# Graph layer with a residual and a layer norm: VectorE instead of ScalarE copies products of picked rows, placing ahead of the network layer, 64 picked columns per engine and pair of runs

## The chip, the cores and the metric

The kernel runs on one core of one Trainium2 chip. The metric is the device time of one execution in microseconds; a lower one is better. The engines are TensorE (PE, with its weight loads as PEld), VectorE (DVE), ScalarE (ACT), GpSimd (POOL) and SyncE (SP).

## The reference

There are N = 12,500 nodes with 128 features and E = 412,500 directed edges, sorted by their destination. Each edge has four attributes (edge_attr) and eight radial values (edge_scalar_attr).

```
f0 = x0 @ W1_0e / sqrt(32);  f1 = einsum(x1, W1_1o) / sqrt(32)       # per node: 32 scalars, 32 vectors
feat, self = halves of f0 and f1
e0, e1 = feat0[edge_src], feat1[edge_src]                            # rows picked per edge
h = gelu(gelu(radial @ W_mlp1 / sqrt(8)) @ W_mlp2 / sqrt(64))        # per edge: 8 -> 64 -> 64
w00, w01, w10, w11 = h @ Wp_..                                       # 4 x 32 weights per edge
mid = products of w.., e0, e1 and the edge's attributes
n = segment_sum(mid, edge_dst) / sqrt(32)
y = cos * self + sin * (n @ W2 / sqrt(64))
out = layernorm(x + y)                                               # fp32 throughout
```

## The kernel before, in words

The edges are cut into 806 runs of 512 edges (four columns q of 128). Two runs are a *pair* (403 of them, index p), two pairs a *chunk* (202, index c); k = 0 or 1 is the pair's place in its chunk. After a preparation (features of all nodes go to a table in HBM, and x stays transposed in SBUF as xT), one loop over the pairs does everything. The order of PE, ACT, DVE and SP instructions is written out by hand, in the order of the Python code (a manual schedule); the engines run their own lists in order and wait for each other by semaphores. Steps of different pairs are interleaved: while VectorE forms the products of pair p, the networks run for chunk c + 2 and the sums of chunk c - 1 are placed.

In the loop, for pair p:

- `gather` (L223, POOL): for the pair nine ahead, each of the eight columns of 128 rows of the table comes by one indirect DMA into a tile G. There are ten such tiles, so a gather waits for the products of pair p - 1. Some columns come in other ways: `aid` (SP, L208) fetches a column of every 14th run row by row, and *picked* columns are made on the chip.
- *Picked rows.* `copy_columns` copies single columns of xT, at addresses that were read into registers, into a 128x128 tile gt: on VectorE (L188) and on ScalarE (L192), each with its own tile. When a tile is full, `picked_rows` multiplies it by the weights wf (L197, PE, into a PSUM tile of the name h), and ScalarE copies the product into column q of G for the run two pairs ahead (L198). `SLOTS` says how many columns an engine copies at which place of the pair: VectorE has three places, ScalarE four, in pairs with k = 0 and k = 1. Which run gets a product is worked out from the running sums of SLOTS. The function `picks` does one place.
- `segments(p - 1)` (L670, PE) sums the products of the pair before over windows of destinations; `segments_kept` (L676, ACT) copies them out of PSUM as sg.
- `weights(p + 1)` (L597, PE): the per-edge weights of the next pair.
- `mlp1` in pairs with k = 0 and `mlp2` with k = 1 (L554, L570, PE; eight matmuls in the program, two passes each in the profile), with their GELUs on ScalarE (L559, L576), two a layer; `show` (L632, ACT) puts edge attributes into the PSUM bank m between the two GELUs of the first layer.
- `place(c - 1)` for k = 0 (L693 and L697, PE): adds the sums of a chunk's four windows into the same bank m; `add` (L710, DVE) adds that to the node sums acc. `move_sums` (L428, ACT) shifts these sums when a group of 512 nodes is done.
- `messages` (DVE): the products M of a pair in three instructions, part 0 (L650) and parts 1 and 2 (both L654), with picks between them. `select` (L639, DVE, for k = 1) makes the windows S from the shown attributes.
- Groups of nodes that are done go through `moments`, `statistics` and `normalise`.

PSUM tiles of the name h have two buffers, shared by the networks, the products of picked rows, transposes and moments; a matmul into one waits until the tile two before it was read.

Of the kernel before, what the change touches and what calls it, by code (L numbers as in the profile page):

```python
# [8 lines left out]
F32 = mybir.dt.float32  # L9
# [3 lines left out]
AF = mybir.ActivationFunctionType  # L13
OP = mybir.AluOpType
PE = mybir.EngineType.PE
ACT = mybir.EngineType.Activation
DVE = mybir.EngineType.DVE
# [4 lines left out]
P = 128  # L22
# [8 lines left out]
PR = 2  # L31
# [14 lines left out]
AID_FROM = 36  # L46
AID_LEAD = 16
STEPS = 12
SLOTS = {DVE: ((24, 20, 20), (24, 16, 28)), ACT: ((12, 16, 16, 12), (12, 16, 16, 12))}
FROM = {DVE: 6, ACT: 6}  # L50
COL_Q = {DVE: Q - 2, ACT: Q - 3}
A_OF = (1, 2, 3, 0)
# [5 lines left out]
def gnn_kernel(ctx: ExitStack, tc: tile.TileContext, x, src, dst, ea4, ea8, w1_0, w1_1, wm1, wm2,  # L58
# [8 lines left out]
    nc = tc.nc  # L67
# [111 lines left out]
    def copy_columns(e, columns):  # L179

        for at, r in columns:
# [9 lines left out]
            else:  # L191
                nc.scalar.activation(to, col, AF.Copy)  # L192

    def picked_rows(e, i):

        pt = ps.tile([P, P], F32, name="h")
        nc.tensor.matmul(pt, GT.pop((e, i)), wf, start=True, stop=True)  # L197
        nc.scalar.activation(G[picked[e][i]][:, COL_Q[e], :], pt, AF.Copy)  # L198

    def aid(s, t):  # L200

# [387 lines left out]
    def weights(p):  # L589

        c, k = divmod(p, CH // PR)
        runs = [i for i in range(PR) if p * PR + i < NS]
        WP[p] = ps.tile([P, PR, Q, P], F32, name="w")
        for q in range(Q):
            for i in runs:
                rows = slice(i * HID, (i + 1) * HID)
                nc.tensor.matmul(WP[p][:, i, q, :], H2[c][q % 2][rows, k, q // 2, :], wpb[rows, :],  # L597
                                 start=True, stop=True)
# [87 lines left out]
    def place(c):  # L686
        ns = min(CH, NS - c * CH)
        b, r = divmod(c, P)
        _, at = nc.values_load_multi_w_load_instructions(
            run_first[b][r:r + 1, :], engines=[PE], min_val=0, max_val=4 * (SPAN - W),  # L690
            skip_runtime_bounds_check_because="bounded above")
        ST[c] = pt = bank[:, :4 * SPAN].rearrange("p (a n) -> p a n", a=4)
        nc.tensor.matmul(pt.rearrange("p a n -> p (a n)"), none[:, :P], none, start=True, stop=False)  # L693
        to = pt.bitcast(U8)
        for k in range(ns):
            k_at = at[k].with_bounds(guaranteed_mod_val=0, out_of_modulus=4)
            nc.tensor.matmul(to[:, :, bass.ds(k_at, 4 * W)].bitcast(F32), SG[c][:, k, :],  # L697
                             PL[c][:, k, :].rearrange("p (a n) -> p a n", a=4), start=False, stop=k == ns - 1)
# [243 lines left out]
    with tc.manual_schedule(engines={PE, ACT, DVE, SP}):  # L942
# [57 lines left out]
        def picks(e, p, i, op=None):  # L1000
            if p < FROM[e]:
                if op:
                    op()
                return
            n = SLOTS[e][p % (CH // PR)][i]
            if not op:
                copy_columns(e, fetch(e, n))
                return
            first = fetch(e, n // 8 * 4)
            op()  # L1010
            copy_columns(e, first + fetch(e, n - n // 8 * 4))

        for p in range(NP):
            c, k = divmod(p, CH // PR)
            mine = [s for s in range(p * PR, (p + 1) * PR) if s < NS]
            if p:
                for s in mine:
                    if s + LEAD - PR < NS:
                        gather(s + LEAD - PR)
            if k == 1 and c + EDGES_AHEAD < NCH:  # L1020
                load_edges(c + EDGES_AHEAD)
            for s in mine:
                if s % P == P // 2 - 16 and (s // P + 1) * P < NS:
                    load_raws(s // P + 1)
                if s % P == P // 2 and (s // P + 1) * P < NS:
                    load_indices(s // P + 1)
                if s % ET == 8 and s - 8 + ET < NS:
                    load_attributes(s // ET + 1)
                for t in range(P // ROWS):
                    a = s + AID_LEAD - t * STEPS // (P // ROWS)  # L1030
                    if a in aided:
                        aid(a, t)
            nets = c + 2 < NCH
            if k == 0:
                placing(c)
                if c + 1 < NCH:
                    hot_rows(c + 1)
            if p:
                segments(p - 1)
                picks(ACT, p, 0, lambda: segments_kept(p - 1))  # L1040
            for e in picked:
                for s in mine:
                    if (e, s + 2 * PR) in pick_of:
                        picked_rows(e, pick_of[e, s + 2 * PR])
            if k == 1 and c + 3 < NCH:
                radial(c + 3)
            cleared = bool(late)
            rest = list(kept)
            norm_kept()
            picks(ACT, p, 1)  # L1050
            if p + 1 < NP:
                weights(p + 1)
            if nets:
                (mlp1, mlp2)[k](c + 2)
                picks(ACT, p, 2, lambda: (gelu1, gelu2)[k](c + 2, 0))
            else:
                picks(ACT, p, 2)
            if k == 0 and c + 1 < NCH:
                show(c + 1)
            for s in mine:  # L1060
                if s % ET == 20 and s - 20 + ET < NS:
                    turn_attributes(s // ET + 1)
            if nets:
                picks(ACT, p, 3, lambda: (gelu1, gelu2)[k](c + 2, 1))
            else:
                picks(ACT, p, 3)
            if k == 0 and c > 0:
                place(c - 1)
                placed = c
            raws_next = [s + PR for s in mine if s + PR < raw_runs]  # L1070
            for s in raws_next:
                turn_rows(s)
            messages(p, 0)
            if k == 0:
                picks(DVE, p, 0)
            messages(p, 1)
            picks(DVE, p, 1 - k)
            for s in raws_next:
                features(s)
            if rest:  # L1080
                norm_rest()
            if cleared:
                new_sums()
                clearing += list(range(4))
            elif clearing:
                clear_sums(clearing.pop(0))
            if k == 1 and c + 1 < NCH:
                select(c + 1)
            if k == 1:
                picks(DVE, p, 1)  # L1090
            messages(p, 2)
            if k == 1 and placed > added:
                add(added)
                added += 1
            picks(DVE, p, 2)
            if k == 0 and 0 < added == c - 1:
                norm(due.get(added - 1, []))
            if p == 0:
                addresses()
                find_first()  # L1100
                new_sums()
                clearing = list(range(4))
            if p == NP - 4:
                count_odd()
# [52 lines left out]
```

## Time and profile before

| | |
|---|---|
| time of three runs, median (lowest to highest) | 5999.37 us (5995.97 to 6003.86) |
| the profiled execution | 5962.68 us, span 5960.8 us |
| granted TensorE clock, mean | 0.65 |
| matmuls (passes) / column copies on VectorE / on ScalarE | 30,231 / 25,984 / 21,888 |
| gathers / products of picked rows (passes) | 2,722 + 72 / 748 |

The profile is of one execution. The page gives the busy time of each engine as a share of the span; "idle before" of a group of instructions is the time in which their engine did nothing just before them, and the name behind the arrow is what ended it. "issue" means that the profile shows nothing that the engine waited for.

### The profile page before, as it was taken

The page shows a single profiled execution, that of the slowest core. Times are in us where ns is not written, and L with a number is a line of the kernel's source. Part 1 is how long each engine was busy: PE and PEld are TensorE (multiplying, and loading weights), DVE is VectorE, ACT ScalarE, POOL GpSimd, SP SyncE. Part 2 cuts the span into 40 slices and gives each one's busy share as a digit, 9 for nine tenths or more (in the row PEclk, how much of TensorE's full clock was granted, in tenths as well). Part 3 has the DMA queues.
Part 4 walks back from the last instruction along what each step waited for, and adds up shares of the span by engine and source line. Part 5 has one row for each costly group of instructions (what it writes and reads, how often), then busy time and mean ns, then how long its engine had stood idle before and what let it go on. Part 6 is the DMA issues. An engine that isn't in the chain of part 4 may idle for free. (4 is left out here: it accounts for less than half of the span.)

```text
span 5960.8 us, 141936 instructions
## 1 busy us (share of the span) xinstructions
PE 3407.7 (57%) x30231; PEld 2603.1 (44%) x30231; DVE 3366.2 (56%) x28706; ACT 3093.4 (52%) x24111; POOL 2636.3 (44%) x2801
## 2 busy tenths in 40 slices
PE   3665655556555555555556555556655555655556
PEld 2544444444444444444444444444434444443444
DVE  1265656555655555656555665566565555665556
ACT  0254555555555555555555555555554555555554
POOL 4344444444444444444444444444444444444441
PEclk5766666666666666666666666666666666666666
DMA  4211111111111111111111111111111111111111
GB/s 100 59 36 40 39 35 38 41 35 43 42 35 39 39 37 43 40 35 36 36 41 37 40 43 38 37 40 40 41 40 35 35 38 38 40 40 34 40 33 23
DMA packets 576979, 239.04 MB, mean 40 GB/s; under 512 B 481402, under 2 KB 526570, under 8 KB 576106
## 3 DMA queue, kind: packets, MB, share of 16 engines
q0 software_dynamic: 89408, 183.29, 10.8%
q1 hardware_dynamic: 465928, 40.14, 5.4%
q10 hardware_dynamic: 20770, 6.47, 0.5%
q14 instruction: 629, 5.15, 0.3%
q8 instruction: 244, 4.00, 0.3%
HBM read 216.86 MB, written 12.99 MB: 39 GB/s over the span
## 5 line engine op out<-in xcount | busy, mean ns | idle before, releaser
L223 POOL DMA_INDIRECT G<-table,idx x2722 | 2567.2, 943 | 3208.9 <-issue 1313.3
L192 ACT ACTIVATE gt<-xT 128x1 f32 x21888 | 2329.1, 189 | 924.5 <-issue 889.3
L188 DVE COPY gt<-xT 128x1 f32 x25984 | 1891.8, 145 | 1565.0 <-issue 1520.5
L670 PE MATMUL seg<-M,S 128*32 128x128 f32 x12896 | 845.7, 371 | 444.2 <-issue 426.8
L597 PE MATMUL w<-wpb,h 64*128 64x128 f32 x6448 | 855.1, 388 | 383.7 <-issue 383.1
L597 PEld LDWEIGHTS w<-wpb,h 64*128 64x128 f32 x6448 | 699.0, 277 | 554.6 <-issue 544.1
L670 PEld LDWEIGHTS seg<-M,S 128*32 128x32 f32 x12896 | 544.3, 148 | 692.1 <-issue 643.3
L654 DVE TENSOR_TENSOR M<-w,G 128x768 f32<-128x768 f32 x806 | 761.1, 945 | 2.7 <-issue 2.7
L676 ACT ACTIVATE sg<-seg 128x256 f32<-128x256 f32 x403 | 151.1, 375 | 1112.3 <-remote 777.6
L697 PEld LDWEIGHTS m<-pl,sg 128*128 128x128 f32 x1612 | 348.6, 312 | 797.7 <-issue 797.7
L693 PE MATMUL m<-none 128*128 128x384 bf16 x202 | 90.8, 450 | 786.1 <-ACT m L632 412.6
L554 PE MATMUL h<-eT,w1b 64*128 64x128 f32 x3232 | 439.3, 403 | 125.8 <-ACT G L198 95.9
L576 ACT ACTIVATE h<-h 128x512 f32<-128x512 f32 x404 | 237.1, 589 | 491.9 <-remote 377.0
L554 PEld LDWEIGHTS h<-eT,w1b 64*128 64x128 f32 x3232 | 394.3, 303 | 159.5 <-ACT G L198 120.5
L570 PE MATMUL h<-h,w2b 64*64 64x256 f32 x3232 | 393.5, 556 | 105.7 <-ACT G L198 68.7
L197 PE MATMUL h<-wf,gt 128*128 128x128 f32 x748 | 244.0, 411 | 268.2 <-issue 154.2
L650 DVE TENSOR_TENSOR M<-w,G 128x512 f32<-128x512 f32 x403 | 275.5, 684 | 204.1 <-remote 73.9
L697 PE MATMUL m<-pl,sg 128*128 128x128 f32 x1612 | 367.5, 404 | 0.0
L197 PEld LDWEIGHTS h<-wf,gt 128*128 128x128 f32 x748 | 162.8, 263 | 403.6 <-issue 246.9
L639 DVE TENSOR_TENSOR S<-oh,m 128x512 f32<-128x512 f32 x202 | 137.2, 679 | 356.7 <-PE m L697 251.4
L559 ACT ACTIVATE h<-h 128x512 f32<-128x512 f32 x404 | 234.6, 581 | 91.0 <-remote 37.9
L570 PEld LDWEIGHTS h<-h,w2b 64*64 64x64 f32 x3232 | 187.5, 186 | 214.9 <-ACT G L198 87.3
(123 smaller groups left out, 1592.5 us busy)
## 6 DMA issues: line engine op xcount, KB each, us to landing
G<-table SPq DMA_DIRECT2D x7040, 0.5 KB
G<-table,idx POOLq DMA_INDIRECT x2722
e<-in_edge_attr SPq DMA_DIRECT2D x201, 64.0 KB
xt<-in_x SPq DMA_DIRECT2D x24, 256.0 KB
table<-ft ACTq DMA_DIRECT2D x24, 256.0 KB
xt<-in_edge_attr SPq DMA_DIRECT2D x24, 256.0 KB
out<-y SPq DMA_DIRECT2D x24, 256.0 KB
xt<-in_dst SPq DMA_DIRECT2D x5, 256.0 KB
```

Of the source, the lines that this page charges most:

```text
L188: nc.vector.tensor_copy(to, col)
L192: nc.scalar.activation(to, col, AF.Copy)
L197: nc.tensor.matmul(pt, GT.pop((e, i)), wf, start=True, stop=True)
L223: nc.gpsimd.indirect_dma_start(out=G[s][:, q, :], out_offset=None, in_=x if s < raw_runs else table, in_offset=bass.IndirectOffsetOnAxis(a ...
L554: nc.tensor.matmul(p1[h][:, j // 2, j % 2, :], w1b[rows, j, :], eT[c][rows, :], start=True, stop=True)
L570: nc.tensor.matmul(p2[r][k * HID:(k + 1) * HID, h * n:(h + 1) * n], w2b[rows, :], H1[c][h][rows, k * n:(k + 1) * n], start=True, stop=True)
L576: nc.scalar.activation(H2[c][r].rearrange("p k j e -> p (k j e)"), P2[c][r], AF.Gelu_apprx_tanh, scale=1.0 / math.sqrt(HID))
L597: nc.tensor.matmul(WP[p][:, i, q, :], H2[c][q % 2][rows, k, q // 2, :], wpb[rows, :], start=True, stop=True)
L650: nc.vector.tensor_tensor(m[:, :, :, :MUL], w[:, :, :2 * MUL].rearrange("p q (a u) -> p q a u", a=2), g[:, :, None, :MUL].to_broadcast([P, ...
L654: nc.vector.tensor_tensor(m[:, :, j, MUL:].rearrange("p q (i u) -> p q i u", i=3), w[:, :, None, (2 + j) * MUL:(3 + j) * MUL].to_broadcast ...
L670: nc.tensor.matmul(SEG[c][q * W:(q + 1) * W, r + i, :], own[:, (r + i) * Q + q, h * W:(h + 1) * W], M[p][:, i, q, h, :], start=h == 0, sto ...
L697: nc.tensor.matmul(to[:, :, bass.ds(k_at, 4 * W)].bitcast(F32), SG[c][:, k, :], PL[c][:, k, :].rearrange("p (a n) -> p a n", a=4), start=F ...
```

## The change

Three things are changed. VectorE instead of ScalarE copies the products of picked rows out of PSUM, and does so behind part 0 of the pair's messages (with k = 1 behind part 1), while the matmuls stay where they were. `place(c - 1)` stands ahead of `mlp1` in the list of TensorE, no longer behind it and behind `show`. And SLOTS gives both engines 64 columns in each pair: VectorE has 64 and 64 (before 64 and 68), ScalarE 64 and 64 (before 56 and 56). With that each engine fills one tile of 128 in each chunk.

```diff
-SLOTS = {DVE: ((24, 20, 20), (24, 16, 28)), ACT: ((12, 16, 16, 12), (12, 16, 16, 12))}
+SLOTS = {DVE: ((24, 20, 20), (24, 16, 24)), ACT: ((16, 16, 16, 16), (16, 16, 16, 16))}
...
+    PT = {}
+
     def picked_rows(e, i):
 
-        pt = ps.tile([P, P], F32, name="h")
+        PT[e, i] = pt = ps.tile([P, P], F32, name="h")
         nc.tensor.matmul(pt, GT.pop((e, i)), wf, start=True, stop=True)
-        nc.scalar.activation(G[picked[e][i]][:, COL_Q[e], :], pt, AF.Copy)
+
+    def rows_kept(e, i):
+
+        nc.vector.tensor_copy(G[picked[e][i]][:, COL_Q[e], :], PT.pop((e, i)))
...
                 picks(ACT, p, 0, lambda: segments_kept(p - 1))
-            for e in picked:
-                for s in mine:
-                    if (e, s + 2 * PR) in pick_of:
-                        picked_rows(e, pick_of[e, s + 2 * PR])
+            products = [(e, pick_of[e, s + 2 * PR]) for e in picked for s in mine if (e, s + 2 * PR) in pick_of]
+            for e, i in products:
+                picked_rows(e, i)
...
             if p + 1 < NP:
                 weights(p + 1)
+            if k == 0 and c > 0:
+                place(c - 1)
+                placed = c
             if nets:
                 (mlp1, mlp2)[k](c + 2)
                 picks(ACT, p, 2, lambda: (gelu1, gelu2)[k](c + 2, 0))
...
                 picks(ACT, p, 3)
-            if k == 0 and c > 0:
-                place(c - 1)
-                placed = c
...
             messages(p, 0)
+            if k == 1:
+                messages(p, 1)
+            for e, i in products:
+                rows_kept(e, i)
+            picks(DVE, p, 0)
             if k == 0:
-                picks(DVE, p, 0)
-            messages(p, 1)
-            picks(DVE, p, 1 - k)
+                messages(p, 1)
+                picks(DVE, p, 1)
```

Lines of the changed kernel: the products' matmul is L199, VectorE's copy of them L203, the placing L698 and L702, messages L655 and L659, S L644, segments L675, sg L681, gathers L228.

## The prediction

> **What bounds the kernel now.** I read the page first, then the groups by line, the waits, and one stretch of the timeline with all engines beside each other.
>
> ```profile
> span 5960.8 us, 141936 instructions
> PE 3407.7 (57%) x30231; PEld 2603.1 (44%) x30231; DVE 3366.2 (56%) x28706; ACT 3093.4 (52%) x24111; POOL 2636.3 (44%) x2801
> ...
> L223 POOL DMA_INDIRECT G<-table,idx x2722 | 2567.2, 943 | 3208.9 <-issue 1313.3
> L192 ACT ACTIVATE gt<-xT 128x1 f32 x21888 | 2329.1, 189 | 924.5 <-issue 889.3
> L188 DVE COPY gt<-xT 128x1 f32 x25984 | 1891.8, 145 | 1565.0 <-issue 1520.5
> ```
>
> No engine is busy more than 57% of the span. The two groups of column copies (gt) are the largest of ScalarE and VectorE, and both have long idle time whose releaser is "issue": the engine waited for nothing that is shown. The timeline says when that is. Its columns: start, length, engine, line, operation, tiles, count, and in brackets the idle time before.
>
> ```profile
> 2996.15 0.94 DVE L654 TENSOR_TENSOR M<-w,G 128x768 f32<-128x768 f32 x1
> ...
> 3008.28 0.38 ACT L676 ACTIVATE sg<-seg 128x256 f32<-128x256 f32 x1 [0.20 <-remote]
> ...
> 3009.41 1.30 DVE L188 COPY gt<-xT 128x1 f32 x20
> ...
> 3010.63 0.95 DVE L654 TENSOR_TENSOR M<-w,G 128x768 f32<-128x768 f32 x1
> ...
> 3012.34 0.94 POOL L223 DMA_INDIRECT G<-table,idx  x1 [6.04 <-issue]
> ...
> 3012.81 0.57 ACT L559 ACTIVATE h<-h 128x512 f32<-128x512 f32 x1
> ...
> 3013.58 0.94 POOL L223 DMA_INDIRECT G<-table,idx  x1 [0.30 <-issue]
> ...
> 3016.64 0.21 DVE L188 COPY gt<-xT 128x1 f32 x2 [0.55 <-issue]
> 3016.70 0.48 PE L693 MATMUL m<-none 128*128 128x384 bf16 x1 [4.13 <-ACT h L559]
> 3016.97 1.91 PE L697 MATMUL m<-pl,sg 128*128 128x128 f32 x8
> 3018.06 0.21 DVE L188 COPY gt<-xT 128x1 f32 x2 [1.21 <-issue]
> 3018.81 1.94 PE L670 MATMUL seg<-M,S 128*32 128x128 f32 x32
> 3019.48 0.22 DVE L188 COPY gt<-xT 128x1 f32 x2 [1.20 <-PE m L697]
> 3019.83 0.94 POOL L223 DMA_INDIRECT G<-table,idx  x1 [0.30 <-issue]
> ...
> 3022.34 0.69 DVE L639 TENSOR_TENSOR S<-oh,m 128x512 f32<-128x512 f32 x1 [0.55 <-issue]
> ...
> 3023.92 0.94 DVE L654 TENSOR_TENSOR M<-w,G 128x768 f32<-128x768 f32 x1
> ```
>
> GpSimd issues the gathers of a pair in a burst, one every 0.94 + 0.30 = 1.24 us (3012.34 to 3019.83, seven). The burst starts 0.8 us after VectorE's last product M of a pair (3011.58), which frees the buffer. Some 3 to 4 us into it VectorE falls to two copies in 1.4 us (3016.64, 3018.06, 3019.48), where it made 20 in 1.30 us before; this ends some 2 us behind the burst. I call it the slow stretch, and there are two in a chunk of two pairs. Outside it VectorE runs nearly without a gap: from 3009.41 to 3011.58 copies and M touch. So VectorE sets the pace, and a chunk here takes 3024.86 - 2997.09 = 27.8 us (ends of the two L654 that close a chunk).
>
> One row in the slow stretch matters for what follows: TensorE made 32 matmuls in 1.94 us at 3018.81, at full rate, after it had stood 4.13 us at L693. An engine that has waited finds its next instructions at hand, so a wait inside the slow stretch costs less than its length.
>
> **The waits the change touches.**
>
> ```profile
> PE m L693 <- ACT m L632: 412.6, 114, 10.9
> ...
> DVE S L639 <- PE m L697: 251.4, 69, 9.3
> ...
> DVE acc L710 <- ACT acc L428: 169.6, 15, 18.2
> ...
> DVE S L639 <- remote: 67.4, 14, 7.1
> ```
>
> TensorE stands at the placing (L693) until ScalarE has written the shown attributes (L632); the segments of the next pair queue behind it; VectorE's S (L639) waits for the placing.
>
> **Part 1, fewer gathers.** Each engine now picks 64 columns in either pair of a chunk, which fill exactly one tile of 128. The changed program has 393 products instead of 374, and 2775 gathers instead of 2794. 19 gathers at 1.24 us are 24 us of bursts; in them the engines made some progress, so between 0 and -24; I take -20.
>
> **Part 2, VectorE's work.** 25,984 columns become 25,216: 768 fewer, at 1.30/20 = 0.065 us, -50 us. It gains 393 copies of 128x128 out of PSUM. The nearest row is its own copy of that shape from the same kind of tile, 279 ns; ScalarE's copy that goes took 257 ns.
>
> ```profile
> L198 ACT ACTIVATE G<-h 128x128 f32<-128x128 f32 x374 | 87.6, 257 | 4.3 <-PE h L197 4.0 <-remote 0.3
> ...
> L479 DVE COPY colv<-h 128x128 f32<-128x128 f32 (+1 forms) x7 | 1.9, 279 | 5.9 <-PE h L478 3.7 <-issue 2.2
> ```
>
> 393 x 0.279 = +110 us, so the part is +60 us where VectorE runs free; nothing (0) if all of it falls into slow stretches, where the supply of instructions is the limit. I take +60.
>
> **Part 3, placing ahead of the network layer.** L693 no longer stands behind ScalarE's L632, so the waits of S, 251.4 + 67.4 = 319 us, can go, and the segments of the second pair can come 4.1 us sooner (the wait at 3016.70). What is late next for S is L632 itself. -319 is one end, 0 the other; S stands at the end of a slow stretch (3022.34), where a wait costs less than its length, and I take a third, -110 us. The 169.6 us at L710 hang on a move of sums on ScalarE that is not moved; 0. The price of the order: the first network layer (16 matmuls) now stands behind the placing, 3018.81 - 3016.70 = 2.1 us, so its GELU on ScalarE (L559, at 3012.81) comes later by about that.
>
> **Part 4, ScalarE's work.** 21,888 columns become 25,088, 16 more in a chunk. A batch of 16 took 1.59 us (row below): +1.6 us a chunk. Two copies of 0.257 go: -0.5 us. ScalarE is off the path as long as nobody waits for its end; it sat idle 777.6 us at L676 alone, and that covers it:
>
> ```profile
> ACT sg L676 <- remote: 777.6, 128, 18.7
> ...
> ACT h L576 <- remote: 377.0, 94, 8.8
> ```
>
> If the cover is gone, it costs 1.1 us a chunk, 199 x 1.1 = 220 us; that is inside part 5.
>
> **Part 5, the new wait.** Now the copy stands on VectorE behind the pair's first M (L650), and it waits for TensorE's products, which wait for the last column of either tile. By the new slot counts ScalarE's tile is full with the very last column of the chunk's second pair. Behind the waiting copy stand 24 columns, then the other M of the pair, whose end starts the next burst. So where does ScalarE's last column lie?
>
> ```profile
> 3025.21 1.59 ACT L192 ACTIVATE gt<-xT 128x1 f32 x16 [0.22 <-issue]
> ...
> 3029.87 0.58 ACT L576 ACTIVATE h<-h 128x512 f32<-128x512 f32 x1
> ...
> 3030.06 0.68 DVE L650 TENSOR_TENSOR M<-w,G 128x512 f32<-128x512 f32 x1
> ...
> 3035.58 0.30 ACT L192 ACTIVATE gt<-xT 128x1 f32 x2 [1.13 <-issue]
> ...
> 3036.57 0.95 DVE L654 TENSOR_TENSOR M<-w,G 128x768 f32<-128x768 f32 x1
> ...
> 3045.93 0.75 PE L197 MATMUL h<-wf,gt 128*128 128x128 f32 x2
> ```
>
> VectorE closed its chunk at 3024.86, ScalarE its own at 3035.88, 11.0 us later, at the end of a slow stretch. The chunk before says the same: 2997.09 against 3008.28 - 0.20 = 3008.08, again 11.0 us. VectorE's copy would be reached at 3030.74. With ScalarE where it is, products at 3035.88 + 0.2 + 0.75 = 3036.8, two copies to 3037.4, 24 columns at 0.065 to 3039.0: the next M would start 2.4 us later than at 3036.57. The first 5 us of the wait cost little, as they lie in the slow stretch; the 2.4 us are real. Against that, ScalarE is no longer held at L676 behind the placing and comes earlier, but it has 1.1 us more to do and its GELU 2.1 us later. With ScalarE earlier by 2.4 us or more the new wait costs nothing: that is the lower end; 2.4 us in each of some 196 chunks, +470 us, the upper. Of ScalarE's idle 777.6 + 377.0 us (5.8 us a chunk) most lies in slow stretches, where work in their place would run slowly too; I count 0.8 of it, 4.7 us, against 1.1 + 2.1 = 3.2 us: earlier by 1.5 us. That leaves 0.9 us a chunk, +176 us.
>
> **Sum:** -20 + 60 - 110 + 176 = +106 us. The profiled execution took 5962.68 us (span 5960.8 and 1.9 around it), which becomes 6069; the median of the runs is 36.7 us more, 5999.37, so I forecast 6105 us.
>
> **Rivals.** *ScalarE comes early enough (faster).* With the segments 4.1 us sooner, ScalarE ends its chunk mostly ahead of the slow stretch, and VectorE's wait for the products is over before the columns behind it could have been supplied. Then -20 + 60 - 110 = -70 us if the row copies run outside slow stretches, and -20 + 0 - 110 = -130 if inside, where VectorE would reach them (3030.74); I take -130, 5870 us. With all of part 3 gained, the far end, it is -20 + 0 - 319 = -339, 5660 us. It decides at a lag of 11.0 - 2.4 = 8.6 us. For it: ScalarE has idle time, and only its last 12 columns, those after the GELU at 3029.87, fell into the slow stretch. Against: there is no slack, as every delay of ScalarE reaches VectorE in the same chunk. The Trainium skill (SBUF — State Buffer, Who interferes with whom) says that TensorE and ScalarE never wait on anyone; by it ScalarE's columns would not slow down during gathers and this case would be certain. The trace disagrees: two columns after 1.13 us of idle at 3035.58.
>
> *The lag stays (much slower).* ScalarE's extra 1.1 and 2.1 us eat all that it gains, and the new wait costs its 2.4 us in each chunk: -20 + 60 - 110 + 470 = +400, 6400 us.
>
> *Nothing visible.* Part 3 pays for part 5: within 12 us of the 5999, 0.2%, which is about what a measurement of this kernel can tell from no change.
>
> **How the numbers follow.** The forecast's case (new wait between 0.4 and 1.8 us a chunk) has 0.43, the faster rival 0.38, the much slower 0.12, no visible change 0.07. So faster 0.38, same 0.07, slower 0.55. The likeliest case's own range is +10 to +280, 6010 to 6280. For 8 in 10 the range takes in the faster rival's price of 5870 with 50 us for more of part 3 (5820), and the much slower one's price of 6400.
>
> **What would show it.** In the profile after: placing (L698) without a wait for ScalarE and S without one for TensorE confirm part 3. VectorE's idle time before L203, released by TensorE's products, is part 5: some 5 us or more a chunk with the other M late confirms it. If instead the lag of ScalarE's last column behind the L659 that closes a chunk is under 8.6 us, the faster rival holds. A slow stretch without gathers in flight, or a pace set by TensorE, would make the whole reading wrong.

## The result, and the profile after

The changed kernel took 6357.97 us (median of four runs, 6354.37 to 6372.16) against 5997.67 us of the kernel before: a ratio of 1.0611, 95% interval 1.0581 to 1.0641, slower by 360 us. The profiled execution took 6359.67 us (span 6357.9), 397 us more than that of before.

First the page of after, then its groups by line (busy time, mean ns of one | idle time before them, what ended it).

```profile
span 6357.9 us, 143359 instructions
PE 3136.6 (49%) x30269; PEld 2286.5 (36%) x30269; DVE 3304.3 (52%) x28329; ACT 3368.0 (53%) x26937; POOL 2625.4 (41%) x2782
```

```profile
L188 DVE COPY gt<-xT 128x1 f32 x25216 | 1747.8, 145 | 1063.6 <-issue 1040.7 <-remote 0.5
...
L681 ACT ACTIVATE sg<-seg 128x256 f32<-128x256 f32 x403 | 153.3, 381 | 1172.8 <-remote 948.9 <-PE seg L675 163.4 <-PE w L602 47.0
...
L644 DVE TENSOR_TENSOR S<-oh,m 128x512 f32<-128x512 f32 x202 | 134.7, 667 | 13.5 <-issue 12.5 <-ACT eT L550 0.7
L203 DVE COPY G<-h 128x128 f32<-128x128 f32 x393 | 113.3, 291 | 1586.9 <-remote 1262.8 <-PE h L199 290.7 <-PE w L602 32.6
...
L698 PE MATMUL m<-none 128*128 128x384 bf16 x202 | 99.8, 494 | 5.9 <-DVE acc L715 4.8 <-issue 1.1
```

VectorE's account explains the difference. Its busy time fell by 61.9 us (3366.2 to 3304.3), its idle time rose from 5960.8 - 3366.2 = 2594.6 to 6357.9 - 3304.3 = 3053.6 us, by 459. The new row copies (L203) have 1586.9 us of idle time before them, 7.9 us in a chunk on average. They only partly take the place of other idle time: the column copies have 501 us less (1565.0 to 1063.6), S 343 less (now 13.5), other groups some 283 less. TensorE waits 5.9 us at L698 (786.1 at the placing of before). That S no longer waits has another cause, told with set 2.

One chunk of the timeline, VectorE, the gathers and the products (start, length, engine, line, ..., in brackets the idle time before):

```profile
3015.14 0.95 DVE L659 TENSOR_TENSOR M<-w,G 128x768 f32<-128x768 f32 x1
...
3016.35 0.95 POOL L228 DMA_INDIRECT G<-table,idx  x1 [3.34 <-DVE M L659]
...
3018.74 0.68 DVE L655 TENSOR_TENSOR M<-w,G 128x512 f32<-128x512 f32 x1
...
3023.44 0.37 PE L199 MATMUL h<-wf,gt 128*128 128x128 f32 x1 [1.05 <-issue]
...
3023.86 0.94 POOL L228 DMA_INDIRECT G<-table,idx  x1 [0.31 <-issue]
...
3026.26 1.31 ACT L192 ACTIVATE gt<-xT 128x1 f32 x13 [1.13 <-issue]
3026.70 0.29 DVE L203 COPY G<-h 128x128 f32<-128x128 f32 x1 [7.29 <-remote]
...
3027.63 0.80 PE L199 MATMUL h<-wf,gt 128*128 128x128 f32 x2 [3.81 <-ACT gt L192]
...
3028.46 0.29 DVE L203 COPY G<-h 128x128 f32<-128x128 f32 x1 [1.46 <-PE h L199]
...
3030.22 1.54 DVE L188 COPY gt<-xT 128x1 f32 x24 [1.47 <-issue]
...
3031.68 0.95 DVE L659 TENSOR_TENSOR M<-w,G 128x768 f32<-128x768 f32 x1
```

VectorE stands still from 3019.41 to 3026.70, nearly the whole slow stretch. The first product ended at 3023.81, and still its copy began only at 3026.70. Then the second copy waits for its product, which had waited for ScalarE's last column (3027.57), then 1.47 us pass in which the addresses of the 24 columns are loaded, and only then the columns run. From the closing M (its end, 3016.09) to this M (start) it takes 15.6 us; the same stretch of before was 11.7 (3024.86 to 3036.57). As a mean over 175 chunks, from the L654 or L659 rows: closing M to the next chunk's first M behind the copies 12.0 us before and 16.2 after, the chunk's middle M to its closing one 13.3 and 11.3.

The experiments ran in seven sets, each on one chip beside runs of the kernel before. The sets are of two kinds: in some the kernel before took 5984 to 6073 us, with the slow stretches of the prediction, in the others 3873 to 3885 us, without any. A ratio holds within its set only.

### The profile page after: what moved, and what is told of

Its sections match the earlier page's. It is cut to its first block, busy times and chain, and to the rows that moved or that the text cites. A ratio compares the mean times of both kernels' runs of the same rounds, so it can differ in the third digit from the quotient of the medians.

```text
span 6357.9 us, 143359 instructions
## 1 busy us (share of the span) xinstructions
PE 3136.6 (49%) x30269; PEld 2286.5 (36%) x30269; DVE 3304.3 (52%) x28329; ACT 3368.0 (53%) x26937; POOL 2625.4 (41%) x2782
## 4 chain that ended last, share of the span: by engine, by line
ACT 31%; PE 26%; issue 16%; another core or an unknown queue 15%; DVE 5%; ACTq 3%; DVEq 1%; DMA 0%; POOL 0%; SPq 0%; POOLq 0%
ACT gt L192 22%; PE w L602 6%; PE h L575 4%; PE m L702 4%; PE h L559 4%; ACTq L174 3%; ACT h L581 3%; PE h L199 3%; ACT h L564 3%; DVE gt L188 3%; PE seg L675 2%; PE h L736 1%; PE m L698 1%; ACT sg L681 1%
## 5 line engine op out<-in xcount | busy, mean ns | idle before, releaser
L228 POOL DMA_INDIRECT G<-table,idx x2703 | 2556.2, 946 | 3612.1 <-DVE M L659 2380.7
L192 ACT ACTIVATE gt<-xT 128x1 f32 x25088 | 2644.2, 189 | 974.1 <-issue 942.4
L188 DVE COPY gt<-xT 128x1 f32 x25216 | 1747.8, 145 | 1063.6 <-issue 1040.7
L575 PE MATMUL h<-h,w2b 64*64 64x256 f32 x3232 | 519.5, 602 | 1284.3 <-ACT eT L550 1258.0
L203 DVE COPY G<-h 128x128 f32<-128x128 f32 x393 | 113.3, 291 | 1586.9 <-remote 1262.8
L199 PE MATMUL h<-wf,gt 128*128 128x128 f32 x786 | 293.2, 448 | 1273.6 <-ACT gt L192 819.8
L675 PE MATMUL seg<-M,S 128*32 128x128 f32 x12896 | 707.5, 346 | 359.3 <-DVE M L659 210.1
L681 ACT ACTIVATE sg<-seg 128x256 f32<-128x256 f32 x403 | 153.3, 381 | 1172.8 <-remote 948.9
L659 DVE TENSOR_TENSOR M<-w,G 128x768 f32<-128x768 f32 x806 | 760.8, 944 | 0.5 <-issue 0.5
L602 PE MATMUL w<-wpb,h 64*128 64x128 f32 x6448 | 711.0, 376 | 40.5 <-issue 40.2
L199 PEld LDWEIGHTS h<-wf,gt 128*128 128x128 f32 x786 | 185.3, 280 | 1418.3 <-ACT gt L192 914.2
L675 PEld LDWEIGHTS seg<-M,S 128*32 128x32 f32 x12896 | 452.2, 137 | 620.7 <-issue 309.1
L602 PEld LDWEIGHTS w<-wpb,h 64*128 64x128 f32 x6448 | 598.7, 269 | 119.0 <-issue 99.4
L702 PEld LDWEIGHTS m<-pl,sg 128*128 128x128 f32 x1612 | 355.8, 307 | 19.7 <-issue 17.4
L702 PE MATMUL m<-pl,sg 128*128 128x128 f32 x1612 | 350.3, 390 | 12.3 <-issue 10.9
L655 DVE TENSOR_TENSOR M<-w,G 128x512 f32<-128x512 f32 x403 | 275.0, 682 | 95.6 <-ACT G L620 58.6
L559 PE MATMUL h<-eT,w1b 64*128 64x128 f32 x3232 | 279.5, 320 | 13.6 <-ACT eT L550 10.2
L559 PEld LDWEIGHTS h<-eT,w1b 64*128 64x128 f32 x3232 | 240.1, 223 | 49.9 <-issue 28.4
L644 DVE TENSOR_TENSOR S<-oh,m 128x512 f32<-128x512 f32 x202 | 134.7, 667 | 13.5 <-issue 12.5
```

The source lines that it names most:

```text
L188: nc.vector.tensor_copy(to, col)
L228: nc.gpsimd.indirect_dma_start(out=G[s][:, q, :], out_offset=None, in_=x if s < raw_runs else table, in_offset=bass.IndirectOffsetOnAxis(a ...
L559: nc.tensor.matmul(p1[h][:, j // 2, j % 2, :], w1b[rows, j, :], eT[c][rows, :], start=True, stop=True)
L575: nc.tensor.matmul(p2[r][k * HID:(k + 1) * HID, h * n:(h + 1) * n], w2b[rows, :], H1[c][h][rows, k * n:(k + 1) * n], start=True, stop=True)
L659: nc.vector.tensor_tensor(m[:, :, j, MUL:].rearrange("p q (i u) -> p q i u", i=3), w[:, :, None, (2 + j) * MUL:(3 + j) * MUL].to_broadcast ...
L675: nc.tensor.matmul(SEG[c][q * W:(q + 1) * W, r + i, :], own[:, (r + i) * Q + q, h * W:(h + 1) * W], M[p][:, i, q, h, :], start=h == 0, sto ...
```

## The experiments

| set | kernel before, us | runs, ratio to it (95% interval) |
|---|---|---|
| 1, no slow stretches | 3876 | rows on ScalarE 1.032 (1.030 to 1.035); placing late 1.025 (1.022 to 1.028); addresses ahead 1.032 (1.030 to 1.034); rows a pair later 0.970 (0.968 to 0.972) |
| 2, slow stretches | 5994 | changed kernel 1.0615 (1.0575 to 1.0656); slots of before 1.0619 (1.0578 to 1.0661); early placing alone 0.988 (0.983 to 0.992); row copies alone 1.073 (1.069 to 1.077) |
| 3, no slow stretches | 3873 | addresses ahead 1.033; rows behind the columns 1.030 (1.027 to 1.033); rows a pair later 0.970; rows on ScalarE 1.031 |
| 4, no slow stretches | 3885 | changed kernel 1.0147 (1.0122 to 1.0171); rows a pair later 0.968 |
| 5, slow stretches | 5984 | rows a pair later, slots of before 1.060 (1.056 to 1.065); rows a pair later, placing late 1.053 (1.048 to 1.057) |
| 6, slow stretches | 6057 | copies outside the slow stretch 0.982 (0.977 to 0.987) |
| 7, slow stretches | 6073 | the wait alone 1.110 (1.105 to 1.115) |

### First theories: slack, ScalarE's columns, or the placing

The first set undid one part at a time. What was expected names three theories: A, VectorE's wait for the products; B, ScalarE's further columns; C, a cost of the early placing.

*Rows on ScalarE* (edit of the changed kernel: in `rows_kept` ScalarE copies, and it is called right behind `picked_rows`):

```diff
-        nc.vector.tensor_copy(G[picked[e][i]][:, COL_Q[e], :], PT.pop((e, i)))
+        nc.scalar.activation(G[picked[e][i]][:, COL_Q[e], :], PT.pop((e, i)), AF.Copy)
```

> The row copies go back to ScalarE, right behind the products; slots and placing stay as changed. Theory A (the loss is VectorE's wait for the products: from the M that closes a chunk to the next chunk's first M behind it took 12.0 us before and 16.2 us after; the early placing gains: from the chunk's middle M to its closing one 13.3 us before, 11.3 us after): the first stretch goes back to about 12 us, the second stays near 11.3, so about 2 us a chunk below the kernel before: 5600 us, 5500 to 5800. Theory B (the 16 further columns make ScalarE the bound): the time stays above 6150 us. Theory C (the early placing costs, since the first network layer and its GELU come later): the time stays above 6150 us and the second stretch is unchanged.

*Placing late* (`place(c - 1)` back behind `show`):

> Placing goes back behind the network layer and the shown attributes; slots and row copies stay as changed. Theory A: the gain of 2 us a chunk is lost, the stretch from the middle M to the closing one goes from 11.3 back to about 13.3 us: 6358 + 200 x 2 = 6750 us, 6550 to 6800. Theory B: 6358 within 50 us. Theory C: below 6250 us.

*Addresses ahead:*

```diff
+            ahead = fetch(DVE, SLOTS[DVE][k][0]) if p >= FROM[DVE] else []
             for e, i in products:
                 rows_kept(e, i)
-            picks(DVE, p, 0)
+            copy_columns(DVE, ahead)
```

> The 24 addresses that VectorE's first batch of columns needs are loaded ahead of the waiting row copies, not behind them; all else as changed. Theory A1 (part of the new cost is that the loads of the addresses stand behind the waiting copy: 1.47 us between the second copy and the first column in the trace): 1.47 us x 200 chunks = 290 us less, 6070 us, at least 100 us less. Theory A2 (the end of the products alone decides, VectorE catches up later): 6358 within 30 us.

*Rows a pair later* (products and copies in the pair ahead of the one that reads them):

```diff
-            products = [(e, pick_of[e, s + 2 * PR]) for e in picked for s in mine if (e, s + 2 * PR) in pick_of]
+            products = [(e, pick_of[e, s + PR]) for e in picked for s in mine if (e, s + PR) in pick_of]
```

> The products and their row copies are made one pair later, still ahead of the messages that read them: ScalarE's last column then lies a pair behind by the time its product is wanted. Placing, slots and the copies' engine stay as changed. Theory A (the missing slack is what costs): VectorE's wait before the row copies falls from 7.9 us a chunk to under 1, the stretch behind the closing M falls from 16.2 to about 12.5 us, 6358 - 200 x 3.7 = 5620 us, 5500 to 5850. Theory B (ScalarE is the bound by its columns): above 6150 us. Theory C (placing): above 6150 us.

Measured: 4002.99, 3974.94, 4001.38 and 3764.03 us, against 3876 of the kernel before. This set has no slow stretches, so the times expected could not come, and these ratios say nothing of the 360 us. The same kernels in set 3 (3998.84 for the rows on ScalarE, 4007.2, 3761.47) and set 4 (3764.19) gave the same ratios, again without slow stretches; so the copies behind the columns, tried there alone, don't speak of them either:

*Rows behind the columns* (`rows_kept` behind `picks(DVE, p, 0)`), 3993.53 us:

> The row copies stand behind the first 24 columns of the pair, directly ahead of the next M, and not ahead of the columns; all else as changed. Theory A (a waiting VectorE gives up what it would have made in the slow stretch, which in the kernel before were just these 24 columns): with slow stretches the wait at the row copies falls from 1587 us to under 900, and the stretch from the closing M to the next chunk's first M behind the copies from 16.2 us to about 13.5: 6360 - 200 x 2.7 = 5820, 5750 to 6050. The forecast's theory (a wait inside a slow stretch costs little, only the late end of the products counts): the copies end when they did, the next M comes 3.0 us sooner at most where the columns went ahead: also below 6360, but the wait stays. Without slow stretches: between 0.98 and 1.02.

What was expected of the repeats, which stay without an answer where slow stretches were meant:

> The addresses of VectorE's first batch of 24 columns are loaded ahead of the waiting row copies; all else as changed. To be read where the slow stretches show (kernel before near 6000 us). Theory A1: the loads are what can't run while the copy waits; between the second row copy and the first column behind it 196 gaps of 1.45 us, 296 us in all, disappear, since the loads trickle in during the wait: 6360 - 296 = 6065 us, 6000 to 6150. Theory A2 (the late end of the products alone decides): 6360 within 60. Without slow stretches: 1.03 again.

> Products and row copies one pair later, behind the chunk's middle M, where the products stand outside the slow stretch. Theory A: with slow stretches the wait of VectorE's row copies falls under 250 us in all, the loss of 430 us goes, what is left is the copies' own 110 less 50 us of columns and the gain of the early placing, 82 us: 5900 to 6050 us. A theory that has VectorE's further work or ScalarE's columns as the cause: 6200 or more. Without slow stretches: 0.97 again.

> Row copies on ScalarE, early placing and the new slots. With slow stretches: as the early placing alone, 0.988, and the slots' own part, which beside VectorE's row copies was nothing (1.0615 against 1.0619): 0.98 to 0.995. Had ScalarE's further columns a price that the waiting row copies covered, up to 1.1 us a chunk, 220 us: 1.02. Without slow stretches: 1.03 again.

### Which part costs, with slow stretches

Set 2 has them, and runs each part by itself. *The changed kernel* again:

> The changed kernel itself, as a reference for the others of this chip. In the profile of before nearly every instruction waited for its supply for half of the time; in the first four experiments, on another chip, no such slow stretch is seen (the kernel before: 3876 us instead of 5998). If the slow stretches are gone here too: Theory A (missing slack of the row copies) expects a ratio between that of the run with the addresses ahead (1.032) and that plus 1.47 us x 200 chunks (290 us, 1.11): 1.05 to 1.08; the theory that the loss comes from the slow stretches alone expects 0.98 to 1.00. If they are there: 1.06 again.

(The profile of before does not show half of the time for nearly every instruction: "issue" is 1520.5 us of VectorE's idle time before its columns, a quarter of the span.)

*Slots of before*, rest as changed (the SLOTS line of the kernel before):

> The slot counts of the kernel before (VectorE 132 columns a chunk, ScalarE 112); rows on VectorE and the early placing stay. ScalarE's tiles then fill at places that move from chunk to chunk, and its products are ready ahead of time in most of them. Theory A (slack): about half or more of the changed kernel's loss goes: ratio 0.98 to 1.03. Theory B (ScalarE's load): the whole loss goes, 0.97 or less. Theory C (the early placing): the loss stays, 1.03 or more, with VectorE's S waiting for the shown attributes.

*Early placing alone* (the kernel before, `place(c - 1)` behind `weights(p + 1)`):

> The kernel before with the early placing alone. Theory A: faster, the stretch from the chunk's middle M to its closing one gets 2 us shorter with slow stretches (5600 us, ratio 0.93) and about as much as ScalarE's slack allows without them (0.97 to 1.00). Theory C: slower by 1 to 3 per cent, S waits for the shown attributes, which stand behind the later GELU.

*Row copies alone* (the changed kernel with the slots of before and the late placing):

> The kernel before with the row copies on VectorE alone (slots of before, placing late). Theory A: VectorE waits for the products of the tiles that fill at the end of a chunk, a part of all: slower by 1 to 3 per cent (without slow stretches), by 2 to 5 with them. Theory B (the loss is ScalarE's columns): within 1 per cent of the kernel before, or faster, since two copies leave ScalarE.

Measured: 6359.69, 6364.5, 5911.84 and 6425.41 us against 5994.17. So the slots are worth nothing here (5 us, within the interval), the early placing gains 82 us alone and 61 beside the row copies (6425 to 6364), and the row copies cost 431 us. Theories B and C fall. Theory A names the right place but missed its numbers: it had 0.93 for the early placing, 0.98 to 1.03 with the slots of before and 2 to 5% for the row copies alone. What it shares with the forecast, that ScalarE's last column decides, does not explain the loss either. With row copies alone VectorE waits as long as in the changed kernel, by the groups of that run:

```profile
L203 DVE COPY G<-h 128x128 f32<-128x128 f32 x374 | 104.6, 290 | 1671.5 <-remote 1292.4 <-PE h L199 311.0 <-PE w L602 59.3
```

but ScalarE's last column there lies at the median 2.4 us behind the closing M, not 11.8 as in before and after. With the slots of before and the early placing it is 2.5 us, and the time is that of the changed kernel. In the changed kernel itself the second copy of a chunk does start right behind its product (0.04 us at the median), which waits for ScalarE; taking that wait away gains nothing.

The waits at S tell where part 3 of the prediction went. Of before, with the early placing alone, and with the row copies alone:

```profile
L639 DVE TENSOR_TENSOR S<-oh,m 128x512 f32<-128x512 f32 x202 | 137.2, 679 | 356.7 <-PE m L697 251.4 <-remote 67.4 <-issue 36.8
...
L639 DVE TENSOR_TENSOR S<-oh,m 128x512 f32<-128x512 f32 x202 | 136.6, 676 | 377.1 <-ACT m L632 192.8 <-ACT h L559 96.5 <-remote 68.0
...
L644 DVE TENSOR_TENSOR S<-oh,m 128x512 f32<-128x512 f32 x202 | 135.1, 669 | 14.2 <-issue 13.0 <-PE m L702 0.6
```

The early placing leaves S waiting as long as before, now for ScalarE. It is the row copies that empty this wait. Their waiting does it, not their work: in set 7, where VectorE has a wait in their place and hardly any work, S waits 9.6 us. From which wait the 82 us of the early placing come is not shown.

A late copy also keeps its PSUM tile, which TensorE needs again two tiles on. That is a rival for the loss. The waits of TensorE for the row copies, at the weight loads of the first network layer in the changed kernel, and at its matmuls with row copies alone:

```profile
PEld h L559 <- DVE G L203: 0.4, 1, 0.4
...
PE h L559 <- DVE G L203: 328.9, 58, 8.5
```

In the changed kernel TensorE hardly waits for the copies, so the tiles don't cause its loss. With row copies alone, and the late placing, they may be a part of the 431 us.

### Late signals

Set 5 moves the wait and finds the reason. *Rows a pair later with the slots of before*, and *with the placing late*:

> Products and row copies one pair later, slots of before, early placing. Theory A with slow stretches: VectorE's wait at the row copies under 300 us in all instead of 1581, and 5900 to 6050 us instead of 6364. Theory of the work (copies and columns make VectorE slower whatever it waits for): 6200 or more. Without slow stretches: 0.97 if the slots do nothing; above 0.99 if the gain of the copies one pair later comes from the columns that moved from VectorE to ScalarE.

> Products and row copies one pair later, placing behind the network layer, new slots. Theory A with slow stretches: some 80 us more than with the early placing, 5980 to 6130 us. Theory of the work: 6250 or more. Without slow stretches: 0.97 to 0.98 if the placing matters little beside them; 1.00 or more if the early placing carries the gain.

Measured: 6347.53 and 6299.29 us against 5984.19, as the theory of the work has it and not as theory A. Theory A falls too: in the first of them the product is made long ahead, and VectorE still waits 1593.4 us at the row copies. The timeline of that run shows why:

```profile
3010.38 1.51 PE L675 MATMUL seg<-M,S 128*32 128x128 f32 x24 [1.88 <-DVE M L659]
3010.59 0.94 POOL L228 DMA_INDIRECT G<-table,idx  x1 [3.41 <-DVE M L659]
...
3011.81 0.80 PE L199 MATMUL h<-wf,gt 128*128 128x128 f32 x2
...
3012.54 2.08 PE L602 MATMUL w<-wpb,h 64*128 64x128 f32 x16
...
3014.27 0.68 DVE L655 TENSOR_TENSOR M<-w,G 128x512 f32<-128x512 f32 x1
...
3016.85 0.94 POOL L228 DMA_INDIRECT G<-table,idx  x1 [0.30 <-issue]
...
3019.15 0.38 ACT L681 ACTIVATE sg<-seg 128x256 f32<-128x256 f32 x1 [6.12 <-remote]
3019.19 0.29 DVE L203 COPY G<-h 128x128 f32<-128x128 f32 x1 [4.25 <-remote]
```

TensorE had ended the segments at 3011.89 and the products at 3012.61, and had gone on to the weights. ScalarE's sg, which waits for the segments, and VectorE's copy, which waits for the product, both start 7.3 and 6.6 us after that, within 0.04 us of each other, 1.4 us after the last gather. "remote" says it: the wait ended by a count of TensorE's semaphore just then, without an instruction that ended near it. The trace records most such counts. Ends of the TensorE instructions that signal, and the recorded counts, in us:

```
this run       ends: L675 3011.88, L199 3012.61, L602 3014.62      counts: 3019.13, 3019.17, 3019.35
changed kernel ends: L675 3006.47, L548 3006.73, L602 3007.82      counts: 3014.32, 3014.36, 3014.55
changed kernel ends: L675 3021.01, L199 3023.81, L199 3028.42      counts: 3026.64, 3026.68, 3028.44
```

In the changed kernel too the first product's signal, of 3023.81, counts at 3026.68, and the copy starts at 3026.70. Over the loop (from the end of an instruction to the next count of its semaphore) 36% of TensorE's signals come over 1 us late in the kernel before, 39% in the changed one, 49% in this run, and 2 to 3% in the changed kernel where there are no slow stretches (set 4). Counts that the trace lacks look late by this measure, but they are few: it has 2501 of 2584 in the changed kernel and 2508 in set 4. Given 3 to 6 us into a burst, 87, 73 and 94% are late in the kernel before (by each us) and 97 to 100% in the changed one; given more than 1 us behind a burst, 0 to 1%. The ends of matmuls are modelled in the trace; that L602 started behind the products at 3012.54 is not.

By the ends of the products, VectorE's wait divides in two. Of the 1587 us in the changed kernel 589 lie ahead of the product's end and 998 behind it; here it is 191 and 1403. With the placing late it is 771 and 467: there the products themselves come late for the copies, as TensorE stands 807.4 us at the placing (for L637) and 433.2 us until VectorE has read the product tiles (at L548).

So theory D: in a slow stretch not only do instructions without a wait come slowly, but a signal from one engine to another mostly arrives only at its end. An engine that has no such wait there goes on slowly; one that has stands until the end. What is shown above is shown of TensorE's signals; of ScalarE's and VectorE's the trace lacks too many counts (one of ScalarE's semaphores has 2154 of 2745). Next, the copies put ahead of the slow stretch:

*Copies outside* (both products behind the first network layer, both in one PSUM tile; copies right behind the last M of the chunk's first pair):

```diff
+            picked_rows(products)          # behind mlp1 and its GELUs, before raws_next
...
             messages(p, 2)
+            for e, i in products:
+                rows_kept(e, i)
```

> The products stand behind the first network layer, and VectorE's row copies right behind the last M of the chunk's first pair, before that M's burst of gathers slows anything; both products lie in one PSUM tile. Early placing, new slots, the number of copies and columns as changed. Theory D (a signal from one engine to another that falls into a slow stretch arrives only at its end, so each wait put there costs the rest of the stretch): with slow stretches VectorE's wait at the row copies falls from 1587 us to under 300, and the time to 5880 to 6050 us: the kernel before, less 82 for the placing, plus 60 for the copies less the columns. Theory of the work (copies and columns cost it wherever they stand): 6250 or more. Without slow stretches 0.95 to 1.00.

Measured: 5943.76 us against 6056.93, 113 us faster than the kernel before. Its groups and timeline:

```profile
L206 DVE COPY G<-h 128x128 f32<-128x128 f32 x393 | 95.9, 286 | 555.0 <-PE h L202 328.4 <-issue 174.1 <-remote 52.4
```

```profile
3010.92 0.95 DVE L662 TENSOR_TENSOR M<-w,G 128x768 f32<-128x768 f32 x1
...
3012.13 0.95 POOL L231 DMA_INDIRECT G<-table,idx  x1 [6.05 <-DVE M L662]
...
3014.04 0.71 PE L202 MATMUL h<-wf,gt 128*128 128x128 f32 x4 [0.74 <-ACT h L567]
...
3014.79 0.49 DVE L206 COPY G<-h 128x128 f32<-128x128 f32 x2 [2.92 <-issue]
```

Here the products end at 3014.75 and the copies start at 3014.79: 2.6 us into the burst the signal is in time, and the segments' signal of 3015.76 is the first that is late (counted at 3021.27). Of the signals of products in this trace 61% count within 0.2 us, and 34% come over 1 us late. What VectorE still waits behind the products' ends is 94 us, where it was 998; the other 461 us of its wait lie ahead of them. With the same copies, columns, slots and placing as in the changed kernel the ratio goes from 1.06 to 0.98. The products stand at another place too and share a tile, so the edit moves more than one wait. The wait did not fall under the 300 us expected (555.0, a third of the 1586.9); the time is as expected. The theory of the work is out.

*The wait alone* (the kernel before; ScalarE's row copies stay):

```diff
+            for pt in waits:                          # the pair's products
+                nc.vector.tensor_copy(speck, pt[:1, :1])
```

> The kernel before, with ScalarE's row copies as they are, and behind the pair's first M (for the second pair of a chunk behind its second M) a copy of one element of each product by VectorE: 374 waits for TensorE, hardly any work. Theory D, with slow stretches: the wait alone costs most of the 431 us that the row copies cost there: 300 to 430 us, ratio 1.05 to 1.07. Theory of the work: 374 x 0.06 = 22 us and the waits hidden, ratio 1.00 to 1.01. Without slow stretches: 1.00 to 1.02.

Measured: 6737.83 us against 6073.07, 665 us slower with hardly any work:

```profile
L1082 DVE COPY speck<-h 1x1 f32<-1x1 f32 x374 | 54.6, 146 | 1900.1 <-ACT G L201 1512.6 <-issue 324.1 <-remote 29.0
```

It is more than the 430 us expected. Here VectorE waits for ScalarE's copy of the product (L201), which stands behind sg and its wait for the segments (1686.9 us with releaser "remote"). A wait in that place is enough to make the loss; this run says nothing of its exact size in the changed kernel.

### The same change without slow stretches

Set 4:

> The changed kernel again. On a chip with slow stretches: 1.06 as before. On one without: the row copies still wait for the products (e4 and e9 stand at 1.03), and the addresses behind them are not hidden: 1.03 to 1.07 by theory A; 1.00 or less if the wait costs only where instructions are starved.

> Products and row copies one pair later. Theory A with slow stretches: VectorE's wait at the row copies under 250 us in all instead of 1587, 5900 to 6050 us. A theory that has VectorE's further work or ScalarE's columns as the cause: 6200 or more. Without slow stretches 0.97 again.

Measured: 3939.53 us against 3885.43 for the changed kernel, and 3764.19 for the rows a pair later. The wait is nearly gone:

```profile
L203 DVE COPY G<-h 128x128 f32<-128x128 f32 x393 | 107.4, 284 | 120.2 <-PE h L199 117.8 <-issue 0.4
```

1586.9 us of waiting become 120.2 and the loss of 6% becomes 1.5%, between the two ranges expected, so most of the loss goes with the slow stretches. Missing slack (theory A) may be a part of what remains: a pair later the rows gain 4.7 points. But these are 175 us, more than the 120 us of wait, so it is not all. Why the edits of sets 1 and 3 that undo or shift one part cost more (1.025 to 1.033) than the whole change (1.0147) is not settled.

## Why the prediction was right or wrong

The direction held and the time lay within the range (6358 in 5820 to 6400), but the size did not: +106 us forecast, +397 in the profiled execution.

- **The step that failed is part 5**, in its sentence that the first 5 us of the wait cost little as they lie in the slow stretch, and only the 2.4 us behind are real. It read the resumption at full rate (TensorE at 3018.81) rightly, but took the wait to cost only what ScalarE's last column adds behind the slow stretch. VectorE's wait lasts to about the end of the slow stretch also where ScalarE is done long before, because the product's signal comes late, and in that time VectorE makes none of the columns that it made there before. The term was +176 with an upper end of 470. Row copies alone cost 431 us, work and waits together, where parts 2 and 5 have 110 (copies) + 176 = 286. That is 145 us of the 259 by which the forecast's +106 falls short of the +365 that set 2 measured; 65 more are the columns and gathers (-70 forecast, -5 measured), 49 the placing (-110 and -61). Moved out of the slow stretch (0.982, in another set), the work has no price that can be seen, so the waits stand for most of the 431.
- **ScalarE's lag** was the wrong thing to watch. It stayed (11.8 us at the median in before and after; a sample chunk has 3027.57 - 3016.09 = 11.5), as the much slower rival had it, and its 6400 us is the nearest price. In the changed kernel the last copy of a chunk does end as that rival says, behind ScalarE's last column. But with row copies alone the lag fell to 2.4 us and the loss was larger, and with the slots of before it fell to 2.5 us while the loss stayed (1.0619). So the rival's number is in part luck: in the chunk shown, the first copy's wait ends 0.9 us ahead of ScalarE's last column (3026.70 and 3027.57).
- **ScalarE's idle time as cover** failed too: 0.8 of the 777.6 + 377.0 us were counted as free. In after sg has 1172.8 us of idle time (before 1112.3), 948.9 of it with releaser "remote", as in the row where it waits for the late signal of the segments. That would also tell why L198 had only 4.3 us of idle time on ScalarE: it stood behind sg, which had waited for the same engine in the same stretch already.
- **The address loads** were left out of the sum. Behind the second copy 1.45 us (median of 196) pass before the columns, 296 us in all. They stand behind the wait in VectorE's queue. Loading them ahead was tried only where no slow stretch is, so what of the 296 us counts there is open.
- **Part 3** had the number nearly right, by luck: -110 forecast, -82 measured alone (-61 beside the row copies). Both marks came, but one for another reason. TensorE's wait at the placing went, as forecast (786.1 us before, 19.5 with the early placing alone). S's wait, of which a third was counted as the gain, did not go by it: 377.1 us instead of 356.7, now for ScalarE's L632, which the prediction itself named as late next, and for the GELU at L559. It went with the row copies.
- **Parts 1, 2 and 4**: columns and gathers, -50 and -20, with ScalarE's own work at nothing, measured together 0 (-5 us, the changed kernel against the slots of before). VectorE's busy time fell by 62 us where the part had it rise by 60; the columns' busy time fell by 144 us (1891.8 to 1747.8), more than 768 columns at 0.065. Columns of a slow stretch take longer each (two in 0.21 to 0.22 us, against 20 in 1.30), and fewer of them may have fallen into one.
- **The Trainium skill's sentence** (SBUF — State Buffer, Who interferes with whom) that TensorE and ScalarE never wait on anyone stands in a section on the ports to SBUF. No run here shows a wait for such a port: the gaps of 1.13 us at 3035.58 have the releaser "issue", and sg's 6.12 us in the rows a pair later are a wait for a semaphore. So that sentence could not have made the faster rival certain, and the traces neither bear it out nor contradict it.

## What to carry to other kernels

Before moving an operation to another engine, look at which waits come with it and at what time of the loop they fall, not only at whose work it becomes: copies of 0.29 us each on VectorE cost 431 us in all, mostly because they brought a wait for TensorE into a stretch in which its signals arrive late, where the old owner was waiting for TensorE anyway. A wait whose releaser is "remote", with several engines starting within 0.1 us of each other, may not be a wait for the work named in the code; compare the end of that work with the start of the waiter before taking the work as its price. Try a moved wait at another place of the loop before giving the move up: the same copies right behind the M that ends the pair left the kernel 1.8% faster than before, where it had been 6% slower (the early placing, which is in both, gains 1.2% alone). And test a mark by the part that it is meant for: S stopped waiting, but not by the placing.

## What the hardware showed that was not expected

- TensorE's signals to other engines arrive late during bursts of indirect gathers, in the sets with slow stretches: counts of TensorE's semaphore 7.3, 6.6 and 4.7 us after the instruction (3011.88, 3012.61, 3014.62), all within 0.22 us, 1.3 us after the last gather. Why some signals given in the first us of a burst are late too is open: some 80% are in the changed kernel, 17% in the kernel before, 5% with the copies outside.
- The slow stretches are not a property of the kernel: the kernel before takes 5984 to 6073 us in four sets and 3873 to 3885 in three, with the same gathers at the same pace (one in 1.25 us, at the median, in both). Sets 4 and 5 ran on a chip of the same number, one without and one with them. What sets them on was not found. Gathers in flight alone do not: in set 4 GpSimd is busy 67% of the changed kernel's span, and here 41%. The traces with slow stretches also lack many counts of the DMA queues' semaphores (24,332 are recorded in the changed kernel's, 61,032 in that of set 4, the same program); whether the recording has a part in the slow stretches or only suffers from them is open. No version was measured in both kinds of set that wins in both: the copies outside were run with slow stretches only (0.982); the rows a pair later gain without them (0.968 to 0.970) and lose with them in its two variants (1.053 and 1.060).
